# A graph layer on one core: hop matmuls in batches of eight by width, the edge MLP's first layer as two row halves, column tiles in turn, and seven shared PSUM banks

## The chip, the cores and the metric

The kernel runs on one core of a Trainium2 chip. A core has a matmul engine (TensorE, PE in the profile), VectorE (DVE), ScalarE (ACT), GpSimd (POOL), and SyncE (SP), which here only starts transfers. They run beside each other and wait for each other through semaphores. Matmul results go to PSUM, eight banks of 128 partitions x 512 float32 each; VectorE and ScalarE take them from there. The metric is the device time in microseconds (us), as the median of several runs. One further execution was profiled; all durations come from it.

## The reference

The input is a graph of 12500 nodes with 64 features and 400000 edges, sorted by destination, with 32 features on each edge. The destinations are crowded at the low node numbers (a uniform number squared).

```python
x_t = mlp2(x, W1n, b1n, W2n, b2n)              # 64 -> 128 -> 64, leaky ReLU
e_t = mlp2(edge_attr, W1e, b1e, W2e, b2e)      # 32 -> 64 -> 64
agg = segment_sum(x_t[src] * e_t * dp_scale, dst)
out = layernorm(x + agg * res_w) * gamma + beta
x   = layernorm(x + out)
# two hops over the graph with its loops, both degrees by the destination
row, col = concat(src, loops), concat(dst, loops)
w = rsqrt(deg[row]) * rsqrt(deg[col]);  h = x
for _ in range(2):
    h = segment_sum(w[:, None] * h[col], row)
x = layernorm(x + h @ W.T + b)
```

So the first half gathers a row for each edge, multiplies it by an edge value, and adds up by destination; the second half goes twice from destinations back to sources.

## The kernel before, in words

**Search and node table** (the first 110 us or so): the kernel finds where the edges of each node begin, computes x_t for all nodes and stores it as a table in HBM.

**Phase 1** (to about 6350 us) is one loop over 261 quads of twelve chunks of 128 edges, from the last quad to the first. In each turn `take` starts twelve indirect gathers of x_t rows on GpSimd, one for each chunk (L553, `xg`, four buffers), and the load of the quad's edge features (L565, `eat`). `xg` thus lets the gathers of a quad start when the messages of the quad four before it are done. The quad's arithmetic is a list of small units: two of `hidden` (L568 to L582), two of `message` (L584 to L606), one `level1` (L608) and one `level2` (L637), each for a different quad of the pipeline:

- `hidden(q, h)`: `eat` holds four superchunks of 32 features on 128 partitions. A matmul with the 128-row weight `w1ab[:, h]` (half of whose rows are zero) gives the first layer of two superchunks (`pw`, L574, float32, which the hardware runs as two passes); ScalarE adds the bias (`z`, L575); after the second half, VectorE applies the leaky ReLU (L577).
- `message(q, h)`: a bias matmul (L588) and three float32 matmuls (L590) give the second layer in `pe`; VectorE multiplies it with the gathered rows (L598, `msg`).
- `level1`: twelve float32 matmuls (L623) with 32-column one-hot operands add the twelve chunks' messages into `pl`, the four column tiles holding one superchunk of three chunks each; ScalarE copies it (`tot`, L632).
- `level2`: matmuls with one-hot operands (L652) add `tot` to a PSUM ring of the open windows of 128 nodes.

Between the units the loop puts work from two generators. `adjacency` counts the edges between all nodes as a dense matrix, 4 destination rows at a time: one-hot operands on VectorE (`oh`, L836), a matmul for each slot of 128 edges (L839, `pa`, 391 columns), whose output is 128, 64 or 32 partitions wide, conversion to 8 bits on ScalarE (L851/L853, `stage`), and a store. `hop1` does the first hop with these counts once they are stored: for a supergroup of up to 14 windows and each of 25 column steps of 512, `hop_mms` (L1025) adds up, for each window, one 128-wide matmul (L1033, the upper two of three 16-bit parts of the operand) and one 64-wide (L1045, the third part) on the lower or the upper column tile; ScalarE copies the sum (`hev`, L1084), and `combine` (L1137) transposes and folds it with matmuls, which VectorE adds to `hacc` (L1142). Each such step returns a cost to the loop, which hands out `H_RATE` = 4400 of it for each quad, in equal parts after the units; `adjacency` gets a share so that it ends a few quads ahead. The units are traced at a higher priority, and a scheduler that works with modelled durations sets each engine's final order. After `adjacency` has ended, `scatter_store` prepares tables for the second hop for 30 quads (L980, L996).

The PSUM banks are assigned by pools (L498 to L503): three for `pa`, and one each for `pw`, `pe`, the ring, `hacc_p` and the shared `pc`/`pl`.

**Phase 2** (about 6450 us to the end) is the second hop. The nodes below window 72 go through the dense counts: 25 column steps, 9 tiles of 8 windows, again with `hop_mms` (accumulator `acc`), then an eviction and matmuls with W (`po`, L1455). The edges of the others, 39 quads, go through GpSimd: a gather, matmuls (L1343), an eviction by ScalarE (`tot`, L1350), and 461 scatters that add rows to four tables in HBM (L1352). At the end the tables are read, added, and the last norm runs over 13 blocks (L1488 to L1506).

The hop's inner order before, in the words of the code:

```python
for i in range(0, n, 2):
    mms.append(lambda i=i: hm(i, first and i == 0))
    if i + 1 < n:
        mms.append(lambda i=i: (lw(i), lw(i + 1)))
        mms.append(lambda i=i: hm(i + 1, False))
```

`hm` is the wide matmul of a window and `lw` the narrow one.

Of the kernel before, what the change touches and what calls it, by code (L numbers as in the profile page):

```python
# [15 lines left out]
I32 = mybir.dt.int32  # L16
# [6 lines left out]
N = 12500  # nodes  # L23
E = 400000  # edges
# [5 lines left out]
MAGIC = 12582912.0  # 1.5 * 2**23: adding it rounds to an integer  # L30

# [1 line left out]
SCC = 3  # chunks in a superchunk  # L33
QC = 4 * SCC  # chunks in a quad
# [13 lines left out]
RING = 7  # windows that add up in a PSUM bank at a time  # L48
LNW = 4  # windows in a node stage

# [6 lines left out]
ER = 128  # edges in a run of the search  # L57
NRUN = E // ER
NCAND = 36  # runs where a slot's first edge is expected
EXT = 130  # edges beyond the last that a slot may reach for  # L60
STG = 8  # blocks in a store
MAXDUP = 16  # counts up to this are exact in FP8
NBIG = 48  # blocks whose row sums may be large though no count is
SC = 512  # src columns in a step of a hop
# [3 lines left out]
def _share(n):  # L68
    """The expected share of the edges before node n."""
    return math.sqrt(n / N)  # L70


def _plan_slots():
    """For each block of 4 nodes: the nodes in a group, and the slots of 128 edges of each group."""
# [18 lines left out]
def _plan_windows():  # L93
    """For each quad, the windows where its nodes are expected."""
# [15 lines left out]
# hop supergroups: windows [lo, hi), from the last to the first  # L110
# [7 lines left out]
# In the second hop, what the nodes from window W0 on hold is scattered edge by edge.  # L118
W0 = 72
Q0 = min(q for q in range(NQ) if QWIN[q][1] >= W0)  # L120
SROWS = (NW - W0) * P  # their rows in a table, after a row of zeros
DW = 8  # windows in a tile of the dense part
HT = 4  # accumulation tables, so that successive scatters don't wait for each other
TROWS = NPAD + P  # their rows: the nodes, then a spare one for each partition


def _slot_tables():
    """The slots in the order of use, 128 to a batch: (block, group, index in group, last?)."""
    slots = []
    for k in range(NBLK - 1, -1, -1):  # L130
        _, w, caps = BLOCKS[k]
        for g in range(4 // w):
            for j in range(caps[g]):
                slots.append((k, w, g, j, j == caps[g] - 1))
    return slots
# [4 lines left out]
SB4 = 4  # batches that are prepared together  # L140
# [3 lines left out]
def _first_run(n):  # L144
    """The first of the NCAND runs where the first edge of node n is expected."""
    p = _share(n)
    e = E * p - 6.5 * math.sqrt(E * p * (1 - p)) - 2
    return min(max(int(e // ER), 0), NRUN - NCAND)


def slot_runs():
    """[P, NSBP, NCAND]: the runs where each slot's first edge is expected."""
# [6 lines left out]
def shape_tables():  # L159
# [9 lines left out]
    # the run before the candidates, and how many of them may begin before the slot  # L169
# [15 lines left out]
def tile_fast(  # L185
    ctx: ExitStack,
    tc: tile.TileContext,
    flag: bass.AP,  # [1, 1] I32 in SBUF: set where the general path has to follow
    xpad: bass.AP,  # [NPAD, D]
    xT: bass.AP,  # [2 * D, NPAD // 2]: the nodes' first and second half  # L190
    srcs: bass.AP,  # [NSEG, P, SEGC]: a column for each chunk of 128 edges
    dsts: bass.AP,
    dstn: bass.AP,  # the dst of the following edge
    base: bass.AP,  # [NSEG, SEGQ * 4]: the first dst of each superchunk
    base4: bass.AP,  # [4, NQ]
    qlo: bass.AP,  # [1, NQ]: the first and the last dst of each quad
    qhi: bass.AP,
    runs: bass.AP,  # [NRUN, ER]: dst
    cand: bass.AP,  # [P, NSBP, NCAND]: the first dst of the runs where each slot is expected
    edges: bass.AP,  # [E + EXT, 2]: src and dst  # L200
    slotT: bass.AP,  # [P, NSBP]: the first node of each slot
    slotJ: bass.AP,  # its first edge among the group's
    slotE: bass.AP,  # the node after the group, for its last slot
    slotR: bass.AP,  # the run before its candidates
    slotLo: bass.AP,  # between these is the number of candidates that begin before it
    slotHi: bass.AP,
    winlo: bass.AP,  # [1, NQ]: the first and last node of each quad's windows
    winhi: bass.AP,
    srcrow: bass.AP,  # [NQ, P * QC]: src, the chunks of a quad next to each other
    ea: bass.AP,  # [NQ, P, SCC * P]: four superchunks of ED rows  # L210
# [12 lines left out]
    WT: bass.AP,  # [D (in), D (out)]  # L223
    b: bass.AP,
    out: bass.AP,  # [N, D]
# [16 lines left out]
    keep = ctx.enter_context(tc.tile_pool(name="keep", bufs=1))  # L242
    gp = keep.tile([P, NW, 3, D], BF16, name="gp")  # the hops' operand in three exact parts
# [7 lines left out]
    # what the general path has to be run for: any value above 0.5  # L251
# [11 lines left out]
    with tc.tile_pool(name="srch", bufs=2) as srch, tc.tile_pool(  # L263
        name="srch1", bufs=1
    ) as srch1, tc.tile_pool(name="ps0", bufs=4, space=PSUM) as ps0:
# [302 lines left out]
    def hidden(q, h):  # L568
        def f():
            if h == 0:  # L570
                hs[q] = edgep.tile([P, 2, SCC * P], F32, name="z")
# [1607 lines left out]
```

## Time and profile before

| | |
|---|---|
| median of three runs | 7554.35 us (7472.85 to 7557.66) |
| span of the profiled execution, first to last instruction | 7540.9 us |
| mean granted TensorE clock | 0.806 |
| PE busy | 5666.7 us, 75% |
| DVE, ACT, POOL busy | 45%, 31%, 54% |
| gathers L553 | 3125 of 1017 ns, 3177.1 us |
| slot matmuls L839 | 6054, 1485.3 us busy |
| hop matmuls L1033 and L1045, first hop | 2425 each, 893.7 and 607.6 us busy |
| hop matmuls L1033 and L1045, second hop | 1800 each, 569.7 and 412.4 us busy |
| first edge layer L574 | 1044 passes, 538.7 us busy |
| level 1 L623 | 6264 passes, 417.7 us busy |

The profiled execution's own time is its span and the start and end around it; the median lies 13.5 us above the span. A row of the groups gives busy time, mean duration of one instruction, and after the bar the idle time just before the group's instructions with what ended it. The slices divide the span in 40 parts, a digit being a busy share in tenths; PEclk is the clock that the throttle granted to TensorE. Matmuls overlap, and so busy times of neighbours aren't added, but starts are compared. In a timeline, a row is a run of like instructions: start, time from the first start to the last end, engine, line, operation, operands, number, and in brackets the idle time before it.

### The profile page before, as it was taken

What the parts mean: (1) busy time and instruction counts of PE and PEld (TensorE: products, weight loads), DVE (VectorE), ACT (ScalarE), POOL (GpSimd) and SP (SyncE); (2) the same over time, 40 slices, a digit from 0 to 9 for tenths busy, and PEclk for the clock granted to TensorE, in tenths of its full rate; (3) what the DMA queues carried; (4) which work ended last, traced back from release to release, by engine and by line L of the source; (5) the groups of instructions that cost most, each with busy time, mean ns of one, the idle gap of its engine ahead of it and who ended that gap; (6) DMA issues with size and microseconds to landing.
All of it is one profiled execution on the core that took longest, in us unless ns stands there. A gap on an engine that the chain in (4) does not pass through costs nothing.

```text
span 7540.9 us, 92485 instructions
## 1 busy us (share of the span) xinstructions
PE 5666.7 (75%) x31668; PEld 2964.0 (39%) x31668; DVE 3363.9 (45%) x10667; ACT 2346.2 (31%) x7842; POOL 4066.1 (54%) x3755
## 2 busy tenths in 40 slices
PE   4566777788787877777677777778677767888898
PEld 2333433444343444444333344444344445322332
DVE  4455444546545445455454555555565424200103
ACT  1455444534333334344343333222221112100100
POOL 5555555555444544554445455555564553588883
PEclk6677888788877887888778778888887865988999
DMA  3444444434333333333333333323222223766666
GB/s 88 119 97 92 97 96 92 97 88 98 85 82 79 87 86 83 88 88 88 71 85 82 89 76 81 81 72 78 69 53 51 65 68 92 180 124 128 120 124 178
DMA packets 1257267, 697.12 MB, mean 92 GB/s; under 512 B 617516, under 2 KB 1188880, under 8 KB 1255760
## 3 DMA queue, kind: packets, MB, share of 16 engines
q1 hardware_dynamic: 1085312, 561.97, 28.7%
q0 software_dynamic: 171472, 129.15, 10.9%
q8 instruction: 250, 4.10, 0.2%
q14 instruction: 233, 1.91, 0.1%
HBM read 489.18 MB, written 201.59 MB: 92 GB/s over the span
## 4 chain that ended last, share of the span: by engine, by line
PE 54%; another core or an unknown queue 14%; issue 12%; POOL 9%; DVE 4%; ACT 4%; DMA 1%; DVEq 0%; SPq 0%; ACTq 0%; POOLq 0%
PE pa L839 13%; PE hacc_p L1033 9%; POOL hop_tab L1352 8%; PE hacc_p L1045 6%; PE pe L590 5%; PE pw L574 5%; PE pl L623 4%; ACT stage L853 3%; PE pc L1137 3%; PE ring L652 2%; DVE oh L836 2%; PE pe L588 2%; PE acc L1033 1%; PE pa L996 1%
## 5 line engine op out<-in xcount | busy, mean ns | idle before, releaser
L553 POOL DMA_INDIRECT xg<-xt_tab,si x3125 | 3177.1, 1017 | 3023.8 <-issue 910.7
L836 DVE TENSOR_SCALAR oh<-iota_b,colT 128x391 bf16<-128x391 bf16 x6054 | 1712.9, 332 | 1685.3 <-PE pa L839 727.7
L853 ACT ACTIVATE stage<-pa 128x391 fp8e4<-128x391 f32 x3077 | 1507.1, 505 | 1925.8 <-PE pa L839 861.7
L839 PE MATMUL pa<-oh,koh 128*64 128x391 bf16 (+2 forms) x6054 | 1485.3, 410 | 725.0 <-issue 382.9
L839 PEld LDWEIGHTS <-koh 128*64 128x64 bf16 (+2 forms) x6054 | 717.5, 178 | 1186.1 <-issue 942.4
L1033 PE MATMUL hacc_p<-at,gp 128*128 128x512 fp8e4 (+1 forms) x2425 | 893.7, 428 | 192.7 <-ACT hev L1084 105.9
L1352 POOL DMA_INDIRECT hop_tab<-tot,first x461 | 722.6, 1568 | 140.5 <-issue 137.5
L1045 PEld LDWEIGHTS <-gp 128*64 128x64 bf16 (+1 forms) x4225 | 267.6, 110 | 1139.3 <-issue 1130.2
L574 PE MATMUL pw<-eat,w1ab 128*128 128x384 f32 x1044 | 538.7, 601 | 161.5 <-ACT z L575 80.6
L853 ACT ACTIVATION_READ_ACCUMULATOR stage<-pa 128x1 f32 x3077 | 643.5, 209 | 0.0
L1045 PE MATMUL hacc_p<-at,gp 128*64 128x512 fp8e4 (+1 forms) x2425 | 607.6, 444 | 16.6 <-issue 15.8
L590 PE MATMUL pe<-w,z 128*128 128x128 f32 x3132 | 562.7, 320 | 33.6 <-issue 33.2
L590 PEld LDWEIGHTS pe<-w,z 128*128 128x128 f32 x3132 | 536.9, 233 | 121.1 <-issue 101.8
L1033 PE MATMUL acc<-at,gp 128*128 128x512 fp8e4 (+1 forms) x1800 | 569.7, 394 | 0.0
L1033 PEld LDWEIGHTS <-gp 128*128 128x128 bf16 (+1 forms) x4225 | 296.3, 100 | 622.3 <-issue 586.8
L575 ACT ACTIVATE z<-pw,b 128x384 f32<-128x384 f32 x522 | 304.3, 583 | 600.9 <-PE pw L574 165.2
L623 PE MATMUL pl<-msg,oh 128*32 128x65 f32 x6264 | 417.7, 243 | 77.3 <-issue 66.3
L652 PE MATMUL ring<-tot,oh 128*128 128x65 f32 x1096 | 209.4, 322 | 338.0 <-ACT tot L632 252.2
L1045 PE MATMUL acc<-at,gp 128*64 128x512 fp8e4 (+1 forms) x1800 | 412.4, 411 | 0.0
L613 DVE TENSOR_TENSOR oh<-iota_f,rel 128x384 f32<-128x384 f32 x261 | 145.5, 558 | 592.4 <-remote 366.6
L598 DVE TENSOR_TENSOR msg<-pe,xg 128x384 f32<-128x384 f32 x522 | 289.4, 554 | 240.7 <-remote 116.0
L623 PEld LDWEIGHTS pl<-msg,oh 128*32 128x32 f32 x6264 | 301.1, 120 | 231.2 <-issue 169.2
(214 smaller groups left out, 4206.1 us busy)
## 6 DMA issues: line engine op xcount, KB each, us to landing
adj<-stage SPq DMA_DIRECT2D x390, 391.0 KB
at<-adj SPq DMA_DIRECT2D x97, 896.0 KB
at<-adj SPq DMA_DIRECT2D x144, 512.0 KB
eat<-in_eaq_dram SPq DMA_DIRECT2D x261, 192.0 KB
xg<-xt_tab,si POOLq DMA_INDIRECT x3125
at<-adj SPq DMA_DIRECT2D x96, 256.0 KB
at<-adj SPq DMA_DIRECT2D x24, 832.0 KB
at<-adj SPq DMA_DIRECT2D x24, 768.0 KB
```

What stands on the lines that cost most here:

```text
L553: nc.gpsimd.indirect_dma_start(out=xg[:, i, :], out_offset=None, in_=xt_tab, in_offset=bass.IndirectOffsetOnAxis(ap=si[:, c : c + 1], axis=0),
L574: nc.tensor.matmul(pw, w1ab[:, h, :], eas[q], start=True, stop=True)
L575: nc.scalar.activation(z[:, h, :], pw, AF.Identity, bias=b1)
L590: nc.tensor.matmul(pe[:, :, c, :], z[:, h, c * P : (c + 1) * P], w2, start=False, stop=(c == SCC - 1),)
L623: nc.tensor.matmul(pl[REL * s : REL * (s + 1), :], oh[:, s * SCC + c, :], m[:, s * SCC + c, :], start=(c == 0), stop=(c == SCC - 1), tile_ ...
L652: nc.tensor.matmul(ring[:, w % RING, :], oh[:, (w - lo) * P : (w - lo + 1) * P], tot, start=False, stop=False, skip_group_check=True,)
L836: nc.vector.tensor_scalar(oh, iota_b, colT[:, i % P : i % P + 1], None, op0=ALU.is_equal)
L839: nc.tensor.matmul(pa[rows, :], koh.pop(i), oh, start=(j == 0), stop=(j == caps[g] - 1), tile_position=(0, rows.start),)
L853: nc.scalar.activation(stage[:, u, :], pa, AF.Identity, saturate=True, accum_out=sums[:, u : u + 1],)
L1033: nc.tensor.matmul(acc[:, :w], gp[:kk, lo + i, 0:2, :].rearrange("p t d -> p (t d)"), t[:kk, i, :w], start=start, stop=False, skip_group_c ...
L1045: nc.tensor.matmul(acc[D * h : D * (h + 1), :w], gp[:kk, lo + i, 2, :], t[:kk, i, :w], start=False, stop=False, skip_group_check=True, til ...
L1352: nc.gpsimd.indirect_dma_start(out=hop_tab[(q * QC + i) % HT], out_offset=bass.IndirectOffsetOnAxis(ap=first[:, q - Q0, i : i + 1], axis=0 ...
```

## The change

- **Hop batches** (both hops). `hop_mms` takes up to eight windows at a time: all their 128-wide matmuls, then all their 64-wide ones. A batch is one step of `hop1` and returns 2600, where single steps returned 240.
- **Edge first layer.** `hidden(q)` is one unit and not two: two matmuls over 64 rows each, on the upper and the lower half of the array's rows, into two banks; then the two copies and the leaky ReLU.
- **Column tiles in turn.** In `level1` the loop over the chunks is the outer and that over the superchunks the inner one; the slots of `adjacency`, and the tables that describe them, are ordered likewise, so that neighbouring matmuls go to different column tiles.
- **PSUM.** The ring keeps its bank; the other seven are one pool, from which `pa`, `pw`, `pe`, `pl`, `pc`, `hacc_p` and the tiles of `scatter_prep` are taken in rotation by `bank`.

The comments and docstrings that the new file leaves out change nothing and are not shown.

```diff
 def _slot_tables():
     slots = []
     for k in range(NBLK - 1, -1, -1):
         _, w, caps = BLOCKS[k]
-        for g in range(4 // w):
-            for j in range(caps[g]):
-                slots.append((k, w, g, j, j == caps[g] - 1))
+        for j in range(max(caps)):
+            for g in range(4 // w):
+                if j < caps[g]:
+                    slots.append((k, w, g, j, j == caps[g] - 1))
...
-    psA = main.enter_context(tc.tile_pool(name="psA", bufs=3, space=PSUM))
-    psW = main.enter_context(tc.tile_pool(name="psW", bufs=1, space=PSUM))
-    psE = main.enter_context(tc.tile_pool(name="psE", bufs=1, space=PSUM))
     psR = main.enter_context(tc.tile_pool(name="psR", bufs=1, space=PSUM))
-    psH = main.enter_context(tc.tile_pool(name="psH", bufs=1, space=PSUM))
-    psC = main.enter_context(tc.tile_pool(name="psC", bufs=1, space=PSUM))
+    banks = main.enter_context(tc.tile_pool(name="banks", bufs=7, space=PSUM))
+
+    def bank(shape, name):
+        n = math.prod(shape[1:])
+        t = banks.tile([P, 512], F32, name=name, tag="bank")[:, :n]
+        if len(shape) == 3:
+            t = t.rearrange("p (a b) -> p a b", b=shape[2])
+        elif len(shape) == 4:
+            t = t.rearrange("p (a b c) -> p a b c", b=shape[2], c=shape[3])
+        return t
...
-    def hidden(q, h):
+    def hidden(q):
         def f():
-            if h == 0:
-                hs[q] = edgep.tile([P, 2, SCC * P], F32, name="z")
-            z = hs[q]
-            pw = psW.tile([P, SCC * P], F32, name="pw")
-            nc.tensor.matmul(pw, w1ab[:, h, :], eas[q], start=True, stop=True)
-            nc.scalar.activation(z[:, h, :], pw, AF.Identity, bias=b1)
-            if h == 1:
-                nc.vector.scalar_tensor_tensor(
-                    z, z, SLOPE, z, op0=ALU.mult, op1=ALU.max
-                )
-                del eas[q]
+            z = hs[q] = edgep.tile([P, 2, SCC * P], F32, name="z")
+            ea_q = eas.pop(q)
+            pws = [bank([P, SCC * P], f"pw{h}") for h in range(2)]
+            for h in range(2):
+                rows = slice(D * h, D * (h + 1))
+                nc.tensor.matmul(
+                    pws[h],
+                    w1ab[rows, h, :],
+                    ea_q[rows],
+                    start=True,
+                    stop=True,
+                    tile_position=(D * h, 0),
+                )
+            for h in range(2):
+                nc.scalar.activation(z[:, h, :], pws[h], AF.Identity, bias=b1)
+            nc.vector.scalar_tensor_tensor(z, z, SLOPE, z, op0=ALU.mult, op1=ALU.max)
...
-            pe = psE.tile([P, 2, SCC, D], F32, name="pe")
+            pe = bank([P, 2, SCC, D], "pe")
...
-            pl = psC.tile([P, D + 1], F32, name="pl", tag="pc")
+            pl = bank([P, D + 1], "pl")
             m = msgs[q % 3]
-            for s in range(4):
-                for c in range(SCC):
+            for c in range(SCC):
+                for s in range(4):
                     nc.tensor.matmul(
                         pl[REL * s : REL * (s + 1), :],
...
-            pa = psA.tile([P, FB], F32, name="pa")
-            for g in range(4 // w):
-                rows = slice(g * w * FA, (g + 1) * w * FA)
-                for j in range(caps[g]):
+            pa = bank([P, FB], "pa")
+            for j in range(max(caps)):
+                for g in range(4 // w):
+                    if j >= caps[g]:
+                        continue
+                    rows = slice(g * w * FA, (g + 1) * w * FA)
...
-        for i in range(0, n, 2):
-            mms.append(lambda i=i: hm(i, first and i == 0))
-            if i + 1 < n:
-                mms.append(lambda i=i: (lw(i), lw(i + 1)))
-                mms.append(lambda i=i: hm(i + 1, False))
-            else:
-                mms.append(lambda i=i: lw(i))
+        def batch(i0, i1):
+            for i in range(i0, i1):
+                hm(i, first and i == 0)
+            for i in range(i0, i1):
+                lw(i)
+
+        for i in range(0, n, HB):
+            mms.append(lambda i=i: batch(i, min(i + HB, n)))
         return mms
...
-                acc = psH.tile([P, SC], F32, name="hacc_p")
+                acc = bank([P, SC], "hacc_p")
                 w = min(SC, PITCH - c * SC)
                 for f in hop_mms(acc, tiles.pop(c), *SGS[sg], c, True):
                     f()
-                    yield 240
+                    yield 2600
...
-        pc = psC.tile([P, SC // P, D], F32, name="pc")
+        pc = bank([P, SC // P, D], "pc")
...
-            units += [hidden(order[t], 0), hidden(order[t], 1)]
+            units += [hidden(order[t])]
```

`HB` is 8. `pk`, `pb` and the key transposes take their banks from the same pool; in the second hop the tables for the scatters are prepared in the pool `psC2`.

More of the change, by code (lines that the diff above doesn't have):

```diff
@@ L773, in prepare @@
         for i in range(SB4):
-            pt = psC.tile([P, 2, P], F32, name="pc")
+            pt = bank([P, 2, P], "pc")
             nc.tensor.transpose(pt[:, 0, :], key[:, i, :], ident)
@@ L891, in tile_fast, with scatter_start @@
     spc = {}
-    def scatter_start(pool, psum, psum1):
+    def scatter_start(pool, psum):
         tri = pool.tile([P, P, QC], BF16, name="tri")
@@ L908, in scatter_start @@
         spc.update(
-            pool=pool, psum=psum, psum1=psum1, tri=tri, spare=spare, kofs=kofs, segs={}
+            pool=pool, psum=psum, tri=tri, spare=spare, kofs=kofs, segs={}
         )
@@ L977, in scatter_prep @@
         nc.vector.tensor_mul(low, sel, spc["tri"])
-        pb = spc["psum1"][0].tile([P, QC], F32, name=spc["psum1"][1])
+        pb = spc["psum"]([P, QC], "pb")
         for c in range(QC):
@@ L993, in scatter_prep @@
         for u in range(0, QC, 4):
-            pc = spc["psum"][0].tile([P, 4, P], F32, name=spc["psum"][1])
+            pc = spc["psum"]([P, 4, P], "pk")
             for i in range(4):
@@ L1023, in load_adj @@
         return t
+    HB = 8
     def hop_mms(acc, t, lo, hi, c, first):
@@ L1106, in hop1 @@
             n = min(GB, NW - j0)
-            if j0 // GB % 2:
-                pc = psH.tile([P, GB, D], F32, name="hacc_p")
-            else:
-                pc = psC.tile([P, GB, D], F32, name="pc")
+            pc = bank([P, GB, D], "pc")
             m = P
@@ L1239, in tile_fast @@
                 scatter_start(
-                    main.enter_context(tc.tile_pool(name="spp", bufs=1)),
-                    (psA, "pa"),
-                    (psC, "pc"),
+                    main.enter_context(tc.tile_pool(name="spp", bufs=1)), bank
                 )
@@ L1292, in tile_fast, with bank2 @@
     psT = ctx.enter_context(tc.tile_pool(name="psT", bufs=2, space=PSUM))
+    def bank2(shape, name):
+        return psC.tile(shape, F32, name=name, tag="pc2")
     dense = [(lo, min(lo + DW, W0)) for lo in range(0, W0, DW)]
@@ L1321, in sp_load @@
                 if spc["pool"] is not h2k:
-                    scatter_start(h2k, (psC, "pc2"), (psT, "pt2"))
+                    scatter_start(h2k, bank2)
                 scatter_prep(q, ct, first[:, q - Q0, :])
```

## The prediction, on record before the changed kernel was timed

> **What bounds the kernel now.** I read the busy table first, then the slices, the chain that ended last, the groups with their waits, and then two timelines, because the shares alone name no bound here.
>
> ```profile
> PE 5666.7 (75%) x31668; PEld 2964.0 (39%) x31668; DVE 3363.9 (45%) x10667; ACT 2346.2 (31%) x7842; POOL 4066.1 (54%) x3755
> ...
> PE   4566777788787877777677777778677767888898
> POOL 5555555555444544554445455555564553588883
> PEclk6677888788877887888778778888887865988999
> ...
> PE 54%; another core or an unknown queue 14%; issue 12%; POOL 9%; DVE 4%; ACT 4%; DMA 1%; DVEq 0%; SPq 0%; ACTq 0%; POOLq 0%
> ```
>
> TensorE holds 54% of the chain, but it is busy in only 7 to 8 tenths of the slices, and the granted clock is about 0.8 in most of them: stretches at 1.0 mixed with stretches at 0.5, so I weight full to half clock 60 to 40. In the second hop POOL stands at 8 tenths for four slices: there its 461 scatters, 1.57 us each plus 0.3 between them, run without a break to 7383 us.
>
> Phase 1 (110 to 6350 us) moves 261 quads in about 24 us each. Its two long waits are seen in one timeline, PE first, then DVE, then POOL:
>
> ```profile
> 5825.40 0.96 PE L623 MATMUL pl<-msg,oh 128*32 128x65 f32 x24
> 5826.29 1.26 PE L839 MATMUL pa<-oh,koh 128*128 128x391 bf16 x5
> 5835.73 1.11 PE L652 MATMUL ring<-tot,oh 128*128 128x65 f32 x4 [8.17 <-ACT tot L632]
> ```
>
> ```profile
> 5835.33 0.56 DVE L598 TENSOR_TENSOR msg<-pe,xg 128x384 f32<-128x384 f32 x1 [6.08 <-remote]
> ```
>
> ```profile
> 5831.96 0.94 POOL L553 DMA_INDIRECT xg<-xt_tab,si  x1 [0.30 <-issue]
> 5843.29 0.94 POOL L553 DMA_INDIRECT xg<-xt_tab,si  x1 [10.38 <-DVE chk L879]
> ```
>
> The `pl` matmuls are recorded as over at 5826.4, yet VectorE and ScalarE go on only at 5835.3, 3.4 us after the last of the twelve gathers started. Then POOL waits 10.4 us until TensorE, working again, has produced the next quad's messages (5842.46), which free a gather buffer. So a quad is a gather stretch followed by a TensorE stretch. I split phase 1 at the gathers' records, each stretch reaching 3.3 us beyond its last gather: gathers are in flight 71% of the time, with PE busy 0.657 there and 0.952 outside. Of PE's work, 0.71 x 6240 x 0.657 = 2911 us lies inside and 0.29 x 6240 x 0.952 = 1723 us, or 37%, outside. Only the latter is plainly TensorE's to shorten.
>
> The groups give the bank waits, and a stretch outside the gathers gives the price of an alternation of tile shapes:
>
> ```profile
> L1033 PE MATMUL hacc_p<-at,gp 128*128 128x512 fp8e4 (+1 forms) x2425 | 893.7, 428 | 192.7 <-ACT hev L1084 105.9
> L574 PE MATMUL pw<-eat,w1ab 128*128 128x384 f32 x1044 | 538.7, 601 | 161.5 <-ACT z L575 80.6
> ```
>
> ```profile
> 2992.63 0.82 PE L623 MATMUL pl<-msg,oh 128*32 128x65 f32 x18
> 2993.38 0.34 PE L588 MATMUL pe<-b2p,ones_b 128*128 128x384 bf16 x1
> ...
> 2994.22 0.81 PE L574 MATMUL pw<-eat,w1ab 128*128 128x384 f32 x2
> 2994.96 0.45 PE L839 MATMUL pa<-oh,koh 128*64 128x391 bf16 x2
> 2995.24 0.38 PE L1045 MATMUL hacc_p<-at,gp 128*64 128x512 fp8e4 x2
> 2995.56 0.60 PE L1033 MATMUL hacc_p<-at,gp 128*128 128x512 fp8e4 x2
> 2996.09 0.41 PE L1045 MATMUL hacc_p<-at,gp 128*64 128x512 fp8e4 x2
> 2996.43 0.60 PE L1033 MATMUL hacc_p<-at,gp 128*128 128x512 fp8e4 x2
> 2996.97 0.41 PE L1045 MATMUL hacc_p<-at,gp 128*64 128x512 fp8e4 x2
> ```
>
> Durations of neighbours overlap, so cost is read from start to start: a pair of windows takes 0.85 to 0.88 us, of which 0.34 for two 64-wide matmuls and 0.54 for two 128-wide ones.
>
> [...] medians at full clock are 0.226 us from a wide hop matmul to the next, 0.309 from wide to narrow, 0.003 between the two narrow ones, and 0.336 back to wide, so a change of width costs 0.08 to 0.11 us. [...]
>
> **The change, part by part** (phase 1, full clock first; the medians at half clock are about twice as long, so the mixed clock is 0.6 + 0.4 x 2 = 1.4 times the full one).
>
> Hop batches. Before, two windows cost 0.226 + 0.309 + 0.003 + 0.336 = 0.874 us, eight 3.50. Batched: 7 x 0.226 + 0.309 + 3p + 0.336, p being the step from a narrow pair to the next on the same tiles. The trace has no such pair in the hop; it is no less than 0.226, and 0.35 is the dearest that `pa`'s narrow pairs suggest (0.28 for 391 columns, scaled to 512). I take 0.32: 3.19, saving 0.31 (0.22 to 0.59). Six windows save 0.21, four 0.10. The 97 windows of 25 column steps are 175 eights, 125 sixes, 50 fours: 54 + 26 + 5 = 85 us, 120 mixed. In the compiled order of the changed kernel a third of the eights are broken up by other work, but changes of shape between the hop and its neighbours also fall (881 to 645, and within the hop 2143 to 391). I take 120, ends 70 and 280.
>
> Edge first layer. Before, 0.74 us for each half (2994.22 to 2994.96), 1.48 a quad; two passes of 0.32 each. After, overlapping row tiles would give 0.64; if they run one after the other nothing is saved, and the compiled order shows 664 changes of shape around `pw` against 256, 408 x 0.1 x 1.4 = 57 us more. Net between -57 and 0.84 x 261 x 1.4 - 57 = 250. No row tile is in the trace; I take 70, near the low third.
>
> Level 1. Eighteen passes in 0.75 us; in the medians the step between fp32 matmuls is 0.089 us on the same tile and 0.057 on another (0.128 and 0.108 at half clock). Eight of eleven steps change: 261 x 8 x (0.6 x 0.032 + 0.4 x 0.020) = 57 us. Changes of shape around `pl` fall from 1082 to 585: 497 x 0.1 x 1.4 = 70. Together 110, rounded down as some were also counted at the hop (60 to 127).
>
> Adjacency slots in turn. Neighbouring narrow slots on the same tile fall from 289 to 16; at 0.16 to 0.28 against 0.003 to 0.30, at most 0.2 each: 30 us (0 to 70). The key tables and counts are as before.
>
> Seven banks in one rotation. PE waits on ACT for a bank 195 us at `pa` (the trace's waits), 106 at `hacc_p`, 81 at `pw`: 382. Counted in the compiled orders, waits with under 2 us of PE work between the eviction's matmul and the next use fall from 1617 to about 1000, by 40%: 150 us (0 to 382). The added waits are at `pe`, which waits for ACT 455 times where it waited for VectorE's message multiply; behind it on TensorE stand the message matmuls, and behind these POOL's gathers.
>
> No DMA is added or moved to another queue; GpSimd's gathers and scatters keep their number.
>
> Sum in phase 1: 120 + 70 + 110 + 30 + 150 = 480 us of TensorE time. What lies outside the gathers counts in full, what lies inside at 0.3, a choice between 0 and 1, as engines there mostly wait for completions: 0.37 + 0.63 x 0.3 = 0.56, so 269 us. In the second hop the scatters hide everything until 7383; in the compiled order some 430 windows follow the last scatter's matmul, 54 eights x 0.31 = 17 us, of which I take 12, because the final norms run beside them. The span becomes 7540.9 - 281 = 7260. The median shown, 7554.35, stands 13.5 above the span: **7273**, taken as 7275.
>
> **The rivals.** (a) *Hidden.* The gather stretch and the late completions set the pace, since the instruction count is unchanged. For it: 71% of phase 1, and the 8.17 us wait above. Against: POOL's own 10.4 us waits for TensorE. At 0.2 of 480, with the 12, it is 108: 7446, within 2%. That the scheduler scatters the batches ends here too.
>
> (b) *Decoupled.* The rotation lets TensorE run on while evictions are late, so messages come before the gathers end. Then work and bank waits count at 0.8 of 330 + 382: 570 us, 6985. For it: the 195 us at `pa`; against: the late completions hold every eviction, and seven banks last only some 3 us of work.
>
> (c) *Slower: the shared rotation stalls the messages.* Before, `pe` had its own bank, and its waits for it came to 17 us. Now its bank comes free when ScalarE has evicted another tile, and ScalarE is held up to 10 us in a gather stretch; a batch of sixteen matmuls (3.2 us, 5.5 at half clock) may stand before it as well. Each us of delay ahead of L588 stops the gathers by one. It decides from (281 + 151) / 261 = 1.7 us a quad; at 2.2 it is 574 - 281 = 293 us slower: 7845. Against: at least 1.6 us of work lies between in nine of ten such waits.
>
> **How the numbers follow.** Forecast 0.52, with its own range 7130 to 7400; (a) 0.20; (b) 0.15; (c) 0.13. The range leaves out (c) and the far part of (b), 0.2 together: 7010 to 7560. About 2%, 151 us, is what a measurement of this kernel can tell from no change; the three runs of before differ by 1.1%. Faster than 7403: 0.67 from the forecast and (b), and nothing of (a); within 2%: 0.20; slower: 0.13.
>
> **What would show it.** Right: hop matmuls in runs of eight, 0.23 us apart and with pairs about 0.32 apart; two `pw` matmuls of a quad in under 1.3 us; waits on ACT at `pa` under 150 us; POOL's waits between gather stretches shorter by about 1 us a quad, their length inside unchanged. Wrong: a large wait on ACT ahead of the `pe` matmuls (rival c), or gather stretches themselves growing as PE is denser, or a lower granted clock[...].

## The result, and the profile after

The changed kernel takes 7501.23 us (median of 20 runs, 7443.4 to 7578.28), beside 7554.91 us for the kernel before: ratio 0.9927, with a 95% interval of 0.9902 to 0.9953. It is 0.7% faster where 3.7% was forecast. The time lies inside the stated range, 7010 to 7560, which is wide enough to hold rival (a) too, and it lies nearest to that one, 7446. Ratios here compare only executions in the faster of the two states that a program shows, and so are not quite the quotients of the medians.

The page of the changed kernel, its busy times, slices and chain (lines moved by some 15: the hop's matmuls are L1050 and L1062, `pw` L583, `pl` L636, the gathers L561, the scatters L1368):

```profile
span 7515.9 us, 92554 instructions
...
PE 5264.4 (70%) x31668; PEld 2925.8 (39%) x31668; DVE 3340.0 (44%) x10667; ACT 2315.4 (31%) x7842; POOL 4020.8 (53%) x3755
...
PE   4655677787777767755677577757557667867897
POOL 5456444555544555454344545545554554488884
PEclk6677777787777778766677677778767776888998
...
POOL 8%; PE 4%; issue 3%; DMA 1%; DVE 1%; ACT 0%; SPq 0%; ACTq 0%; POOLq 0%; DVEq 0%
```

TensorE is busy 402 us less, at a mean granted clock of 0.756 against 0.806, and the span is only 25 us shorter. (The chain is followed here only back through the second hop, so it says nothing of phase 1.) The busy times by stretch put both changes in phase 1. Columns: the stretch, its length, busy us of PE, PEld, DVE, ACT and POOL with the number of instructions, granted clock, DMA share, GB/s. First the kernel before, then the changed one:

```profile
110.00:6350.00 6240.00, 4569.55 (x25237) 2535.62 (x25237) 3130.26 (x10175) 2212.37 (x7560) 3222.92 (x3173) 0.79 0.35 83
```

```profile
110.00:6350.00 6240.00, 4284.16 (x25174) 2441.84 (x25175) 3088.74 (x10143) 2175.16 (x7549) 3161.03 (x3162) 0.74 0.37 83
```

Nearly the same instructions were done in the same 6240 us, with 285 us less of busy TensorE at a lower clock. The first and the last scatter of the second hop, first in the kernel before, then in the changed one:

```profile
6473.72 1.62 POOL L1352 DMA_INDIRECT hop_tab<-tot,first  x1 [0.30 <-issue]
...
7381.41 1.55 POOL L1352 DMA_INDIRECT hop_tab<-tot,first  x1 [0.30 <-issue]
```

```profile
6475.05 1.62 POOL L1368 DMA_INDIRECT hop_tab<-tot,first  x1 [0.30 <-issue]
...
7380.82 1.55 POOL L1368 DMA_INDIRECT hop_tab<-tot,first  x1 [0.30 <-issue]
```

The first starts at 6473.7 us before and at 6475.1 after: phase 1 gained nothing in these two executions. The 25 us come from the end: from the last scatter to the end of the span it is 160 us before and 135 after. The medians differ by 53.7 us; where the other 29 come from, one profile of each kernel can't say.

The work itself became cheaper by more than forecast. One timeline of TensorE in the changed kernel shows it, and also what became of it:

```profile
2983.66 0.55 PE L636 MATMUL pl<-msg,oh 128*32 128x65 f32 x24
...
2985.57 1.05 PE L583 MATMUL pw<-eat,w1ab 64*128 64x384 f32 x4
2986.55 0.88 PE L665 MATMUL ring<-tot,oh 128*128 128x65 f32 x6
...
2989.01 1.89 PE L1050 MATMUL hacc_p<-at,gp 128*128 128x512 fp8e4 x8
...
3001.50 0.44 PE L854 MATMUL pa<-oh,koh 128*64 128x391 bf16 x1
3011.35 1.65 PE L583 MATMUL pw<-eat,w1ab 64*128 64x384 f32 x2 [9.41 <-issue]
...
3023.19 3.62 PE L1050 MATMUL hacc_p<-at,gp 128*128 128x512 fp8e4 x8
```

Level 1's 24 passes (the trace has two for each float32 matmul, 6264 for the 3132 of level 1) take 0.55 us, where eighteen took 0.75; both halves of the edge layer take 0.98 us to the next start, where one took 0.74; eight wide hop matmuls take 1.89 us at 2989 and start 0.216 us apart. Then TensorE stands still for 9.41 us, with two of the edge layer's four passes done before the wait and two after it. The next eight, at 3023, take 3.62 us and start 0.427 us apart: the granted clock is 1.0 in the first eight and 0.5 in these. GpSimd and VectorE of the changed kernel in the same stretch:

```profile
2984.59 1.48 POOL L561 DMA_INDIRECT xg<-xt_tab,si  x1 [3.57 <-DVE oh L851]
...
3015.96 0.94 POOL L561 DMA_INDIRECT xg<-xt_tab,si  x1 [0.31 <-issue]
3031.55 1.01 POOL L561 DMA_INDIRECT xg<-xt_tab,si  x1 [14.65 <-DVE oh L851]
```

```profile
2992.21 0.56 DVE L611 TENSOR_TENSOR msg<-pe,xg 128x384 f32<-128x384 f32 x1 [0.23 <-PE pe L603]
...
3011.09 0.56 DVE L626 TENSOR_TENSOR oh<-iota_f,rel 128x384 f32<-128x384 f32 x1 [13.14 <-remote]
...
3028.64 0.56 DVE L611 TENSOR_TENSOR msg<-pe,xg 128x384 f32<-128x384 f32 x1 [3.43 <-PE pe L603]
```

Gathers follow each other from 2984.6 to 3016 us. VectorE stops at 2998 for 13 us and TensorE at 3002 for 9.4; both start again at 3011, with further pauses until about 3020, 4 us after the last gather's start. The next gathers follow only after the two messages at 3028.6 and 3030.7. I laid all stretches of eleven to thirteen gathers over each other (181 before, 176 after) and took TensorE's busy share and granted clock in single us from the stretch's first gather:

```
us from first gather      2     6     10    14    18    22
before  PE busy          0.98  0.87  0.60  0.41  0.93  0.99
before  granted clock    0.90  0.96  0.89  0.73  0.58  0.74
after   PE busy          0.91  0.73  0.52  0.41  0.93  0.98
after   granted clock    0.92  0.90  0.71  0.63  0.60  0.74
```

The changed kernel's TensorE falls off sooner, to 0.73 at the sixth us where it was 0.87, and stands at the same point when the gathers end. That it has by then run out of work that it may do is my reading of this.

### The profile page after: what moved, and what is told of

It is laid out like the page before. It is cut to its first block, busy times and chain, and to the rows that moved or that the text cites. A ratio compares the mean times of both kernels' runs of the same rounds, so it can differ in the third digit from the quotient of the medians.

```text
span 7515.9 us, 92554 instructions
## 1 busy us (share of the span) xinstructions
PE 5264.4 (70%) x31668; PEld 2925.8 (39%) x31668; DVE 3340.0 (44%) x10667; ACT 2315.4 (31%) x7842; POOL 4020.8 (53%) x3755
## 5 line engine op out<-in xcount | busy, mean ns | idle before, releaser
L561 POOL DMA_INDIRECT xg<-xt_tab,si x3125 | 3125.3, 1000 | 3058.7 <-DVE oh L851 1212.0
L1050 PE MATMUL hacc_p<-at,gp 128*128 128x512 fp8e4 (+1 forms) x2425 | 794.8, 465 | 118.2 <-issue 51.3
L1368 POOL DMA_INDIRECT hop_tab<-tot,first x461 | 719.8, 1561 | 140.5 <-issue 137.8
L1050 PEld LDWEIGHTS <-gp 128*128 128x128 bf16 (+1 forms) x4225 | 438.1, 113 | 733.8 <-issue 441.4
L868 ACT ACTIVATION_READ_ACCUMULATOR stage<-pa 128x1 f32 x3077 | 705.0, 241 | 0.0
L583 PE MATMUL pw<-eat,w1ab 64*128 64x384 f32 x1044 | 504.5, 700 | 237.2 <-issue 158.8
L1050 PE MATMUL acc<-at,gp 128*128 128x512 fp8e4 (+1 forms) x1800 | 459.1, 393 | 13.1 <-DMA at<-adj 12.3
L1062 PE MATMUL hacc_p<-at,gp 128*64 128x512 fp8e4 (+1 forms) x2425 | 429.2, 413 | 38.3 <-issue 37.5
L636 PE MATMUL pl<-msg,oh 128*32 128x65 f32 x6264 | 221.8, 245 | 292.8 <-DVE msg L611 118.0
L1152 PE MATMUL pc<-twoid,hev 128*128 128x64 f32 x1764 | 338.8, 350 | 97.4 <-issue 51.8
L1062 PEld LDWEIGHTS <-gp 128*64 128x64 bf16 (+1 forms) x4225 | 226.3, 113 | 433.1 <-issue 352.2
L1152 PEld LDWEIGHTS pc<-twoid,hev 128*128 128x128 f32 x1764 | 311.2, 260 | 175.3 <-issue 85.4
```

Source lines behind the costliest of these rows:

```text
L561: nc.gpsimd.indirect_dma_start(out=xg[:, i, :], out_offset=None, in_=xt_tab, in_offset=bass.IndirectOffsetOnAxis(ap=si[:, c : c + 1], axis=0),
L583: nc.tensor.matmul(pws[h], w1ab[rows, h, :], ea_q[rows], start=True, stop=True, tile_position=(D * h, 0),)
L868: nc.scalar.activation(stage[:, u, :], pa, AF.Identity, saturate=True, accum_out=sums[:, u : u + 1],)
L1050: nc.tensor.matmul(acc[:, :w], gp[:kk, lo + i, 0:2, :].rearrange("p t d -> p (t d)"), t[:kk, i, :w], start=start, stop=False, skip_group_c ...
L1062: nc.tensor.matmul(acc[D * h : D * (h + 1), :w], gp[:kk, lo + i, 2, :], t[:kk, i, :w], start=False, stop=False, skip_group_check=True, til ...
L1152: nc.tensor.matmul(pc[:m, j, :], ev[:, j * P : j * P + m], twoid, start=True, stop=True)
```

## The experiments

Times are set against the kernel before on the same chip. The five groups of runs came to five chips. On four of them that kernel takes 7394 to 7542 us, as in the first comparison; on that of the second group (`a_traffic`, `a_free`, `a_colsback`, `a_ownbanks`) it takes 5490.

**Without gathers.** In both kernels `gathers` gives one constant tile.

```diff
+    xgc = xgp.tile([P, QC, D], F32, name="xg")
+    nc.vector.memset(xgc, 0.5)
     def gathers(q):
...
-            nc.gpsimd.indirect_dma_start(
...
-        xgs[q] = xg
+        xgs[q] = xgc
```

> The kernel before without its 3125 gathers of phase 1: every message is multiplied with one constant tile, so the messages' values are not those of the reference; all else stays. Theory A (in phase 1 a quad's pace is a gather stretch of about 14 us, then a pause of some 9 us in which late completions and the message follow one another; TensorE's work is not the bound): without gathers phase 1 shrinks from 6240 us to about TensorE's own work, 3730 us at full clock and some 10% for waits, and the kernel takes 5100 to 5600 us, with a granted clock over 0.9. Theory B (TensorE at a clock that the throttle lowers is the bound): the kernel gains little, 7000 us or more.

> The changed kernel without its gathers in the same manner. Theory A: TensorE's work is now the bound, and the change's saving, 3732 to 3268 us at full clock in the two traces, shows: 300 to 480 us (6 to 9%) below the kernel before without gathers, where with gathers it was 0.7%. Theory B: the clock gives the saving back here too: within 2% of the kernel before without gathers.

Measured: 5386.69 us for the kernel before (ratio 0.7147, 0.7131 to 0.7163) and 4892.40 for the changed one (0.6495, 0.648 to 0.6511). Phase 1 by stretch, first the kernel before, then the changed one, both without gathers:

```profile
110.00:4200.00 4090.00, 3943.25 (x25222) 2234.51 (x25222) 3019.28 (x10173) 2212.74 (x7556) 64.02 (x48) 0.96 0.43 101
```

```profile
110.00:3700.00 3590.00, 3322.90 (x25064) 2053.46 (x25063) 2940.39 (x10143) 2111.18 (x7536) 55.45 (x48) 0.95 0.50 114
```

TensorE is busy 96% and 93% at a clock of 0.96 and 0.95, and the change is worth 494 us, 9.2%. So it does what it says, and the gathers hide it: theory A. The gathers cost the kernel before 2155 us and the changed one 2609 (7501.23 - 4892.40, on two chips). A planner that sees no gathers also orders some instructions otherwise, so the pair says what the gathers hide in size, not to the per cent.

The changed kernel without gathers was run once more on another chip, in the group of `a_again` below.

> The changed kernel without gathers (values not the reference's), on the chip of this group. The gathers' effect on the other engines is what differs between the chips: 4890 on either, within 1%. If the other engines differ: elsewhere.

Measured 4886.28 us, within 0.2% of the first. But that chip, too, is one on which the kernel before takes some 7500 us, so this doesn't say whether the other engines differ on the chip of 5490.

**A fifth gather buffer.**

```diff
-    xgp = main.enter_context(tc.tile_pool(name="xgp", bufs=4))
+    xgp = main.enter_context(tc.tile_pool(name="xgp", bufs=5))
...
+        if t + GPRE < NQ:
+            take_ahead(order[t + GPRE])
```

> The changed kernel with five gather buffers for four, gathers started one quad earlier (room for it from one destination index buffer and one one-hot buffer less). Theory A in its first form (the loop from a message to the gathers that it frees sets the pace): POOL's pause after each stretch shrinks by several us, and the time falls by 3% or more, to 7270 or less. Theory A in its second form (what a gather stretch does to TensorE's completions sets the pace, whenever the stretch begins): within 1% of the changed kernel, 7430 to 7570.

Measured: 7545.69 us, ratio 1.0025 (1.0000 to 1.0050): not faster, some 1% slower than the changed kernel by its ratio. The distance between message and gather is not what is short. (The room came from one destination index buffer and one of eleven one-hot buffers, and what their loss costs isn't separated.)

**Gathers that nobody waits for, on two chips.** Messages take the constant tile, the gathers stay, into three buffers in place of four.

```diff
-        xgs[q] = xg
+        xgs[q] = xgc
```

> The changed kernel with all its gathers, but messages take a constant tile and nothing reads what was gathered (values not the reference's): GpSimd needs to wait for no message. If only the loop from message to gather and back sets the pace, the gathers, 3125 of 1.25 us = 3900 us, run beside everything else and the kernel takes 4900 to 5300 us. If gathers in flight hold up the other engines' work whoever waits for them: TensorE does 0.49 us of full-clock work per us under them (2224 of 4585 us in the changed kernel's trace), 1910 of its 3270 us in those 3900 us, and the remaining 1360 need some 1550 us; with 1280 us for start and second hop 6700 us.

> The changed kernel with gathers that no message waits for (values not the reference's), on the chip of this group. On a chip of 7550 us: 4900 to 5300 if only the loop from message to gather sets the pace, about 6700 if gathers in flight hold up the others' work. On one of 5490 us: 5441 again.

Measured: 5441.38 us on the chip of 5490, and 8908.46 us on one of 7502, ratio 1.1871 (1.1789 to 1.1954). The two pages' slices, the faster chip first:

```profile
PE   4866687989889798886988678767897877778987
POOL 7777777777777777777777777777777658888882
PEclk7788898989999899897999888979997688888998
```

```profile
PE   3115162727456372819163644537263539877797
POOL 5771717161523425170716143343534340068884
PEclk6557585858677685959586766768576769688898
```

On the second chip TensorE and GpSimd take turns: where POOL is at 7, PE is at 1 and the clock at 5. In its phase 1, gathers in flight leave TensorE 0.11 us of full-clock work per us (431 in 4050). The same program, with the same gathers 1.25 us apart, has TensorE at 8 tenths on the first chip. So both my numbers were wrong for the second chip: the loop from message to gather, once cut, doesn't free the kernel, it lets the gathers come in longer rows (76 in the 100 us from 2850), and these hold up everything else more: TensorE does 0.11 us of work per us, where the changed kernel's trace has 0.49, and in the 880 us from 120 VectorE is busy 257 us and ScalarE 276, against 615 and 619 on the first chip.

**Traffic in place of gathers.**

```diff
-            nc.gpsimd.indirect_dma_start(
...
+            nc.sync.dma_start(xg[:, i, :], xt_tab[r : r + P])
```

> The changed kernel with each gather replaced by a plain load of as many rows and bytes (128 rows of 256 bytes), started by SyncE into tiles that nothing reads; messages take a constant tile, so their values are not the reference's. If it is the traffic of the gathers that slows the other engines: near the changed kernel, over 6800 us. If it is the gather as GpSimd carries it out[...]: near the changed kernel without gathers, 4890 to 5100 us.

Measured: 5428.75 us, on the chip of 5490 (ratio 0.9883). As that chip hardly shows the hold-up (5490 us for the kernel before), this doesn't answer its question: whether the bytes or GpSimd's way of moving them hold the engines up stays open. The plain loads take as long there as the gathers that nobody waits for, 5441.38, and no kernel without either was run there.

**Parts undone.** Four kernels, each the changed one with one part as before: widths alternating within a batch (`a_pairs`), level 1 and slots in their old order (`a_colsback`), the old sharing of banks (`a_ownbanks`), the edge layer over 128 rows (`a_fullk`).

```diff
-            for i in range(i0, i1):
-                hm(i, first and i == 0)
-            for i in range(i0, i1):
-                lw(i)
+            for i in range(i0, i1, 2):
+                hm(i, first and i == 0)
+                if i + 1 < i1:
+                    lw(i)
+                    lw(i + 1)
+                    hm(i + 1, False)
```

```diff
-            for c in range(SCC):
-                for s in range(4):
+            for s in range(4):
+                for c in range(SCC):
...
-        for j in range(max(caps)):
-            for g in range(4 // w):
-                if j < caps[g]:
+        for g in range(4 // w):
+            for j in range(caps[g]):
```

```diff
-        t = banks.tile([P, 512], F32, name=name, tag="bank")[:, :n]
+        tg = OWN[name]
+        t = own[tg].tile([P, 512], F32, name=name, tag=tg)[:, :n]
```

```diff
-                    w1ab[rows, h, :],
-                    ea_q[rows],
+                    w1ab[:, h, :],
+                    ea_q,
```

> The changed kernel with the hop's matmuls alternating in width as in the kernel before, in batches of the same size and cost. If the removed changes of width lie in time that has no value in phase 1, only the second hop's end sees them: 0 to 0.5% slower than the changed kernel (7500 to 7540). If the batches gave the whole measured gain, 0.7% slower (7555); if batches of one width had brought what the prediction counted, 2% slower (7640).

> The changed kernel with level 1 and the adjacency slots in their order of before. Batches of one width are worth 1.8% by the run with alternating widths, and the whole change 0.7%, so other parts together cost about 1.1%. If the column order is what costs (it interleaves the groups' slots, and the last slot of each group comes late): 7420. If it is worth what the prediction counted at the measured scale (30 + 110 of 480 us): 7520 to 7550. If it doesn't matter: 7501 within 0.5%.

> The changed kernel with the PSUM banks shared out as before: three for pa, one each for pw, pe, the hop and the pc and pl tiles. If the shared rotation stalls the messages (rival c, in small): faster by about 1%, 7420. If the rotation saves waits that have value: slower by 1% or more, 7580 and up. The prediction's 150 us at the measured scale would be 7530.

> The changed kernel with the edge first layer over all 128 rows, as before, but in one unit with two banks. If row halves run one after the other and cost changes of tile shape (408 more around pw): 0 to 1% faster than the changed kernel. If they overlap and count: up to 1% slower. On a chip where the gathers are the bound, no difference over 0.3% either way.

> The changed kernel itself once more, beside the kernel before on the chip of this group of runs, since the last group's chip ran the kernel before in 5490 us and not in 7550. If the chip is one of 7550 us: ratio 0.993 again. If it is one of 5490: there the gathers of a kernel of the same kind followed each other without pauses (3100 in 4370 us), so the saving shows until the gathers are the bound; the free gathers took 5441, so 5440 to 5490, ratio 0.99 to 1.00. If instead TensorE's saving shows in full there, 5000.

Measured: alternating widths 7638.39 us, ratio 1.0110 (1.0064 to 1.0156), against 0.9927 for the changed kernel on another chip: 1.8% slower, as the last of its expectations has it. Its tail after the last scatter is 160 us again, and its phase 1 ends 103 us later. The edge layer over 128 rows takes 7426.39 us, 0.9886 (0.9814 to 0.9958), beside the changed kernel's 7457.33 us, 0.9943 (0.9915 to 0.9971), on the same chip: no difference that these runs can tell. The old column order and the old banks were 1.0112 (1.0091 to 1.0132) and 1.0209 (1.0184 to 1.0234), on the chip of 5490; the changed kernel itself wasn't run there, so what these parts are worth stays open. (With one bank for `pw`, `a_ownbanks` also keeps the two row halves of every quad apart.)

So no single part is shown to cost anything. But the kernel with alternating widths has everything of the change except the order of the widths, and it is 1.1% slower than the kernel before, although TensorE's busy time up to the first scatter, weighted with the granted clock, is 3581 us in its trace against 3858 before. Under the gathers, too, the order of the widths has value, then, and something in the rest of the change costs about as much. Which part it is isn't shown. One candidate that no run separates is the order of the units: the two message halves of a quad are 9 and 65 matmuls apart in the changed kernel, and 39 and 26 in the kernel before.

The hop batches alone, put into the kernel before with the lines of `hop_mms` and the cost of 2600 that the change has:

> The kernel before with the hop batches alone (order and cost of a step), its banks, its two hidden units and its column order kept; the message halves stay 39 and 26 matmuls apart. If the batches bring the whole gain: 0.7 to 1.8% faster than before, as undoing them in the changed kernel made that 1.8% slower. If they need the shared banks: no difference over 0.5%. Slower by 1%, if a batch of sixteen matmuls holds up messages.

Measured: 7364.98 us, ratio 0.9944 (0.991 to 0.9977), its tail 136 us. That is the changed kernel's gain within the intervals: the batches alone bring as much as the whole change, and the shorter end of the second hop is theirs.

**Half gather buffers.** Eight tiles of six chunks, each freed by one message half; in the changed kernel also another order of the units.

```diff
-        xg = xgp.tile([P, QC, D], F32, name="xg")
+        for h in range(2):
+            xg = xgp.tile([P, HC, D], F32, name="xg")
...
-                xgs[q][:, k * h : k * (h + 1), :],
+                xgs[q][h],
...
-            units += [hidden(order[t])]
-        if 0 <= t - 1 < NQ:
-            units += [message(order[t - 1], 0), message(order[t - 1], 1)]
+        units += msg[:1] + hid + msg[1:] + lv1 + lv2
```

(The last line is that of `a_split2`; `a_split` has message 0, hidden, level 1, message 1, level 2.)

> The changed kernel with two gather buffers of six chunks for each of twelve, freed by one message half each, and the units in the order message 0, hidden, level 1, message 1, level 2, so that the halves are 56 and 18 matmuls apart in the compiled order of TensorE (9 and 65 in the changed kernel). If the hold-up grows with the length of a gather stretch (TensorE is busy 0.98 in a stretch's second us and 0.43 in its 17th, in the changed kernel's trace): two shorter stretches lose less, 3 to 8% below the changed kernel, ratio to before 0.92 to 0.97. If it grows with the number of gathers alone: within 1% of the changed kernel, 0.985 to 1.00.

> The kernel before with the same half buffers, its units in their order (message halves 40 and 28 matmuls apart). By the length of the stretch: 2 to 6% faster than before. By the number of gathers: within 1%.

> The changed kernel with half gather buffers and the units in the order message 0, hidden, message 1, level 1, level 2: the message halves are 37 and 35 matmuls apart in the compiled order (56 and 18 in a_split, whose ratio to before was 0.955; 40 and 28 in the kernel before with half buffers, 0.942). If even halves are what counts and the change's smaller TensorE work then has value: ratio 0.90 to 0.935. If the spacing doesn't matter: 0.955 again. If the work saved has no value under gathers even so: 0.94, as the kernel before with half buffers.

Measured: `a_split` 7058.01 us, 0.9552 (0.9462 to 0.9641); `b_split` 6955.12, 0.9421 (0.9308 to 0.9534); `a_split2` 6854.86, 0.9255 (0.9194 to 0.9316). By their ratios all three beat both kernels. An edit that takes no work from any engine is worth 6% in the kernel before, eight times what the change is worth. With the halves 37 and 35 matmuls apart the changed kernel beats the kernel before with half buffers, by 1.8% from chip to chip, with intervals that just touch. That rows of gathers get shorter is only half true: in `b_split` 673 of 3125 gathers come in rows of seven or fewer (20 before), but 1036 in rows of more than fourteen (599 before). (A new row begins here where two gathers start over 3 us apart; the two traces are of two chips.) What fell is GpSimd's time between rows, from the last start of one to the first of the next: 2406 to 1837 us.

**Gathers spread out.** A first try put a small iota after each gather:

> The changed kernel with a small iota on GpSimd after each gather, some 0.4 to 0.5 us, so that gathers are 1.7 us apart and not 1.25. If a backlog of gathers holds the engines up, it doesn't build up: 6300 to 6900 us where the kernel before takes 7500. If gathers in flight hold them up at any rate: 12 x 0.45 us a quad longer, 8500 us or more. On a chip of 5490 us GpSimd is the bound: 3125 x 0.4 us more than 5440, 6500 to 6900.

Measured 8485.98 us, which tells nothing: nothing needs the iota, and the planner put 2794 of them behind phase 1, where they hold up the second hop by about 1200 us. The second try writes into the tile that the gather fills, and so stays ahead of it.

```diff
+            nc.gpsimd.memset(xg[:, i:, :] if i else xg[:, 6:, :], 0.0)
             nc.gpsimd.indirect_dma_start(
                 out=xg[:, i, :],
```

> The changed kernel with a GpSimd memset of 64 to 704 columns ahead of each gather, in the tile that the gather fills, so that it stays ahead of it; on average some 0.4 us. If density holds the engines up (a backlog of gathers): the engines go on under the gathers, and the time falls to 6300 to 7000. If being in flight does: a quad's stretch is 12 x 0.4 us longer and the pause that follows hardly shorter, 8000 to 8700. On a chip of 5490 us for the kernel before: GpSimd is the bound, 6500 to 6900.

Measured: 6654.06 us, ratio 0.9008 (0.8948 to 0.9067), in two runs. GpSimd's timeline and the page's slices:

```profile
3015.41 0.70 POOL L561 MEMSET xg<- 128x704 f32 x1
3016.27 1.01 POOL L562 DMA_INDIRECT xg<-xt_tab,si  x1 [0.16 <-POOL xg L561]
3017.28 0.49 POOL L561 MEMSET xg<- 128x448 f32 x1
3017.93 1.11 POOL L562 DMA_INDIRECT xg<-xt_tab,si  x1 [0.16 <-POOL xg L561]
```

```profile
PE   3776788888888888867887778686577788676997
POOL 5488888888888888888878888888888884888883
PEclk6677788888888888767886888797687867888998
```

Giving GpSimd 1440 us more to do makes the kernel 10% faster than the kernel before. Its gathers now come 1.73 us apart on average, with 42 pauses of over 4 us between starts in place of 214, and TensorE works at 8 tenths beside them: 0.62 us of full-clock work per us, against 0.49 in the changed kernel. So dense rows of gathers hold the engines up on such a chip, not gathers in flight as such. VectorE pays something: its one-hot operands take 453 ns each, where they took 328. The planner's order differs too (message halves 16 and 54 matmuls apart), and no run spreads gathers and halves buffers at once.

## Why the prediction was right or wrong

**The bound.** Right that a quad is a gather stretch and a pause, and that TensorE is held up in the first. Its split doesn't quite add up: 2911 + 1723 is 4634 us, and the trace has 4569.55. Done again over 110 to 6350 us, the stretches take 74% of the time, with TensorE busy 0.67 there and 0.91 outside, and 33% of its busy time lies outside. Wrong that this part is "plainly TensorE's to shorten": the pause begins where the gathers left TensorE, and in it the clock is low, 0.70 before and 0.68 after.

**The step that failed** is the factor 0.56 in the sum for phase 1, which counted work outside the gathers in full and inside at 0.3. Measured from the two traces, busy time weighted with the granted clock: the work under the gathers fell from 2689 to 2224 us, outside it was 1043 and then 1044 (to within 2%, by where one lets a stretch end). The whole saving of 464 us came out of time in which TensorE waits anyway, and phase 1 ended at the same us. The right factor in these executions is 0, which is rival (a) carried to its end; (a) itself still took 0.2. It is a net: the order of the widths brought something there, and something else in the change, still open, took it back. That the prices were too small made up for part of the error by luck: the measured 464 us, at the prediction's 1.4 for the mixed clock and its 0.56, would have been 364 us of forecast gain for the work alone, and not 269 with the bank waits.

The granted clock fell along with this, from a mean of 0.806 to 0.756. In the changed trace TensorE was busy 0.63 (median) in the 6.8 us before a half-clock period and 0.85 before a full-clock one. In the stretch above TensorE stands still for 9.41 us from 3002, the clock is 0.5 from 3004 to 3028, and the eight at 3023 start 0.427 us apart, where those at 2989, at 1.0, start 0.216 apart. That the standing still lowered the clock isn't shown by this. How much of the lost gain is the clock's alone, no run separates.

**The prices**, the edge layer's apart, were too small: an error in the other direction. Eight windows take 7 x 0.216 + 0.309 + 3 x 0.216 + 0.312 = 2.78 us in the changed trace: the narrow pairs' step p is 0.216, not 0.32, and the saving 0.72, not 0.31. The edge layer's pair takes 0.85 us at full clock against 1.50 where its two row tiles start 0.007 us apart in each pass, but they do so in 71 of the 261 quads only. In some 70 more the four passes follow each other less closely (1.32 us), and in 114 other work stands between them, as at 3000 us above. The group as a whole is little cheaper than the 538.7 us of before:

```profile
L583 PE MATMUL pw<-eat,w1ab 64*128 64x384 f32 x1044 | 504.5, 700 | 237.2 <-issue 158.8
```

Up to the first scatter the clock-weighted busy time of TensorE is 3858 us before and 3399 after; 3581 with alternating widths, 3608 with the old banks, 3448 with the edge layer over 128 rows, 3433 with the old column order. So the edge layer saves 49 us, about 70 at the mixed clock, which is what was put, because most pairs don't overlap in full. And the banks, priced for their waits alone, save work as well. Together the work fell by 464 us at full clock, where my 330 us at mixed clock meant 236.

**Bank waits** fell as priced, PE's waits on ACT at `pa`, the hop and `pw` from 382 to some 205 us, 177 where 150 was put, but nothing came of it: TensorE's idle time in phase 1 rose by 285 us. POOL's waits between the rows, too, which were to be about 1 us a quad shorter, went from 2406 to 2453 us. Rival (c) shows as a trace only: waits at `pe` on all engines went from 17 to about 56 us, far from the 1.7 us a quad from which it would decide.

**The second hop's end** had the right mechanism and was mis-sized: 25 us and not 12, as the eights save more than twice as much. The tails of `a_pairs` (160 us) and `b_batch` (136) show it.

**Named and not priced** was the lower granted clock, as what would make the prediction wrong. Rival (b) did not come: with fewer waits for banks the messages came no sooner, as phase 1 shows.

## What to carry to other kernels

Before pricing instructions on an engine that is busy in 75% of the time, take away the neighbour that it takes turns with: a run without the gathers shows what these cost, here 2155 us, over four times what the change saves even there. Work saved on an engine that then waits for the same event was worth next to nothing here (0.7%), and the granted clock fell with it, from 0.806 to 0.756. Look at when a producer may issue, and how densely it does: the same gathers, released by halves (in the kernel before) or spread (in the changed one), were worth eight to fourteen times the change.

## What the runs showed of the hardware that was not expected

- Rows of gathers 1.25 us apart hold the other engines up: in the first comparison TensorE's busy share falls from 0.98 to 0.41 within 14 us of a row's start and comes back 3 to 4 us after the last gather's start; without gathers (`b_nogather`) the same kernel takes 0.7147 of its time. On four of the five chips of the experiments the kernel before takes 7394 to 7542 us, near the 7555 of that comparison. On the fifth it takes 5490, and there they hardly do: one kernel, with TensorE at 8 tenths beside its gathers, took 5441 us on that one and 8908 on another. How a gather holds the others up, and why the chips differ, stays open.
- Spread to 1.73 us apart, the same gathers let TensorE work at 8 tenths (`a_spaced2`).
- Two row-half matmuls in float32 can start 0.007 us apart in each of their two passes, and the pair then costs 0.85 us where one over all rows costs 0.75; in the changed kernel 71 of 261 pairs did.
- A pair of narrow hop matmuls on the column tiles just used by another pair starts 0.216 us after it, the same step as from one wide matmul to the next.
